# A two-layer graph transformer on one core: the first stage's typed projections by exact sort instead of by mask

## The chip, the cores and the metric

The kernel runs on one core of one Trainium2 chip. The core has a matrix engine (TensorE, PE in the profile), VectorE (DVE), ScalarE (ACT), GpSimd (POOL) and SyncE (SP), each with its own stream of instructions, and 16 DMA engines that move data between on-chip memory and DRAM. PEld is the matrix engine's loading of weights. The metric is the device time of one execution in microseconds (us); smaller is better. The kernel before takes 3468.3 us, the median of 9 runs between 3451.37 and 3474.05.

## The reference

A graph of 6250 nodes (128 features each, one of 16 node types) and 100000 edges (one of 32 edge types, sorted by destination) goes through two layers. What matters here is the start of a layer:

```python
def typed_linear(x, t, W):                      # W: 16 x 128 x 128, t: type of each node
    y_all = jnp.einsum('nd,tdo->nto', x, W)
    return jnp.take_along_axis(y_all, t[:, None, None], axis=1)[:, 0]

k = typed_linear(x, ntype, Wk).reshape(n, H, HS)   # H = 8 heads of HS = 16
q = typed_linear(x, ntype, Wq).reshape(n, H, HS)
v = typed_linear(x, ntype, Wv).reshape(n, H, HS)
kT = jnp.einsum('nhd,htdo->nhto', k, Watt)         # for each of 32 edge types
vT = jnp.einsum('nhd,htdo->nhto', v, Wmsg)
kw = kT[src, :, etype]
m  = vT[src, :, etype]
a  = jnp.einsum('ehd,ehd->eh', kw, q[dst]) * pri[:, etype].T / SQRT_D
att = edge_softmax(a, dst, n)
hag = segment_sum(m * att, dst)                    # then a typed linear, SiLU, skip, layer norm
```

After the two layers come a linear map and a last layer norm with a residual.

## The kernel before, in words

Nodes are padded to 49 blocks of 128 (6272 nodes). The program has a prologue, a first stage, and then the edges of layer 0 and of layer 1.

**First stage.** It writes the table `tabs[0]`: for every node and every one of the 32 edge types a row of 256 numbers (the node's k and v, already multiplied by the edge type's matrices). Per block of 128 nodes that is 4 MiB, in two pieces of 2 MiB ("table pieces", tile `st`, one for edge types 0 to 15 and one for 16 to 31, called `tg` 0 and 1), 98 pieces in all. `table_block` (L256) makes them: for each piece two halves (k, then v), for each half four products `tb` of 32 x 512 on TensorE (L268), each of which ScalarE (L275) or VectorE (L273, one in four) copies from PSUM into the piece. There are three `st` buffers. SyncE stores each piece to consecutive rows (L759).

The k and v of a block come from `linears0` (L721), which works on superblocks of 3 or 4 blocks: GpSimd loads the rows `hr` and a broadcast of the types `ntb` (L725, L727), TensorE transposes the rows, and then for each of the 16 types VectorE makes a copy of the superblock with all nodes of other types set to zero (`masked`, L238) and TensorE adds its products with that type's Wk and Wv (L739). So every node is multiplied 16 times for k and 16 times for v, and 15 of those products add zero. `linears0` of the next superblock is a generator: the loop at L755 to L773 takes one or two steps of it after each half of a table block.

**Ranking, beside the first stage.** `rank_order` (L452) is a second generator that the same loop advances. It first counts how many edges each node receives (`degrees`, L333: 46 chunks, each with a large comparison `ol` and a smaller one `oh` on VectorE, L348 and L351, and 17 small bf16 products on TensorE, L355). Then it ranks the nodes by type class and degree (VectorE with TensorE in turn, L457 to L656). Then come the "gathers" (L662 to L677): for each of 13 superblocks of the ranked order GpSimd gathers the edges' table indices `ell` (3 or 4 instructions, L664) and the nodes' rows `xr` (3 or 4, L673), and writes the rows out as `xrd` (L676), for which it first waits until the `xr` rows have landed. In the loop, `degrees` gets one step per half, the ranking two, the gathers one per two halves.

**Edges.** `edges` gathers table rows for the ranked nodes on GpSimd (L987, 1734 gathers over both layers), multiplies and reduces on VectorE, and writes layer 1's table `tabs[1]` with a GpSimd scatter per table piece (L1198, 100 of them) in between. The first gather of layer 0 waits until every piece of `tabs[0]` has landed.

**Order.** TensorE, VectorE, ScalarE and SyncE run their instructions in an order that the framework's scheduler makes from the program. GpSimd's order in the first stage and in the edges is the program's own (`manual_schedule`).

Of the kernel before, what the change touches and what calls it, by code (L numbers as in the profile page):

```python
# [9 lines left out]
F32 = mybir.dt.float32  # L10
# [8 lines left out]
P = 128  # L19
# [75 lines left out]

@with_exitstack
def kernel(
# [43 lines left out]
    PAD = P * EC + P  # L141
    assert D == P and H * HS == D and H == 8 and HS == 16 and EC % J == 0 and NP > N and L == 2
    assert max(KB) * H + P <= 512 and max(KB) <= P and min(KB) >= CH and NR >= NP and NB <= P and TY == NC * TC

# [145 lines left out]
    nti = pp.tile([P, NT], I32, name="nti")  # L290
    nc.sync.dma_start(dsti, dst[0:P])
# [3 lines left out]
    nc.sync.dma_start(nti, ntype.rearrange("(i p) -> p i", p=P))  # L295
# [23 lines left out]

    nc.vector.scalar_tensor_tensor(kvi, srci, float(RT), eti, op0=ALU.mult, op1=ALU.add)  # L320
# [12 lines left out]
    def degrees(got):  # L333

        loi = pp.tile([P, EC], I32, name="loi", tag="lo")
        hii = pp.tile([P, EC], I32, name="hii")
# [110 lines left out]
    with tc.tile_pool(name="tp", bufs=2) as tp, \  # L447
            tc.tile_pool(name="tlin", bufs=1, space=PSUM) as tlin, \
            tc.tile_pool(name="tnb", bufs=5, space=PSUM) as tnb, \
            tc.manual_schedule(engines={mybir.EngineType.Pool}):  # L450

        def rank_order():  # L452
# [231 lines left out]
            for l in range(L):  # L684
                sk = pp2.tile([P, TY], F32, name="sk")
                nc.scalar.dma_start(sk, skip[l:l + 1, :].to_broadcast([P, TY]))
                nc.scalar.activation(sk, sk, AF.Sigmoid)
                oa = pp.tile([P, NB, TY], F32, name="oa", tag="hii")
                nc.vector.tensor_tensor(oa, onehot, sk.unsqueeze(1).to_broadcast([P, NB, TY]),
                                        op=ALU.mult)  # L690
                nc.vector.tensor_reduce(alpha[:, l], oa, axis=AX.X, op=ALU.add)
                nc.vector.tensor_scalar(beta[:, l], alpha[:, l], -1.0, 1.0,
                                        op0=ALU.mult, op1=ALU.add)
                nc.vector.tensor_scalar(alpha[:, l], alpha[:, l], 0.5, None, op0=ALU.mult)
                yield
# [19 lines left out]
            nc.vector.tensor_copy(over, mt_ps[:, 0:1])  # L715
# [5 lines left out]
        def linears0(got, i0, k):  # L721

            n = k * P
            hr = tp.tile([P, SB, D], F32, name="hr")
            nc.gpsimd.dma_start(hr[:, :k], rows(x, i0, k))  # L725
            ntb = tp.tile([P, SB * P], I32, name="ntb")
            nc.gpsimd.dma_start(  # L727
                ntb[:, :n], ntype[i0 * P:i0 * P + n].unsqueeze(0).to_broadcast([P, n]))
            yield
            tr = tlin.tile([P, SB * P], F32, name="l0")  # L730
            for i in range(k):
                nc.tensor.transpose(tr[:, i * P:(i + 1) * P], hr[:, i, :], ident)
            hT = tp.tile([P, SB * P], F32, name="hT")
            nc.scalar.copy(hT[:, :n], tr[:, :n])
            ps = [tlin.tile([P, SB * P], F32, name=f"l{i}") for i in range(2)]
            yield
            for t, xm in masked(tp, range(TY), ntb, hT, n):
                for i in range(2):
                    nc.tensor.matmul(ps[i][:, :n], wkqv[:, i, t, :], xm[:, :n],  # L739
                                     start=(t == 0), stop=(t == TY - 1))  # L740
                yield
            kT, vT = (tp.tile([P, SB * P], F32, name=f"yT{i}") for i in range(2))
            nc.scalar.copy(kT[:, :n], ps[0][:, :n])
            nc.scalar.copy(vT[:, :n], ps[1][:, :n])
            got.append((kT, vT))
            yield

        load_later()


        got, stage = [], ""
        sbs = list(superblocks(NT))
        for _ in linears0(got, *sbs[0]):
            pass
        for s, (i0, k) in enumerate(sbs):  # L755
            beside = linears0(got, *sbs[s + 1]) if s + 1 < len(sbs) else iter(())
            for i in range(k):
                def store(tg, st, b=i0 + i):
                    nc.sync.dma_start(  # L759
                        tabs[0].rearrange("(n g t) c -> g n (t c)", g=TG, t=16)[  # L760
                            tg, b * P:(b + 1) * P, :],
                        st.rearrange("p t c -> p (t c)"))
                for half, _ in enumerate(table_block(tp, tnb, *got[s], i, (1,), 3, store)):
                    next(beside, None)
                    if half % 4 == 3:
                        next(beside, None)

                    if stage != "gathers" or half % 2:
                        stage = next(ranking, None)
                    if stage not in ("degrees", "gathers"):  # L770
                        stage = next(ranking, None)
            for _ in beside:
                pass  # L773
        for _ in ranking:
            pass
# [3 lines left out]
    def arm(fast):  # L779
# [527 lines left out]

        for l in range(L):
# [67 lines left out]
```

## Time and profile before

| | |
|---|---|
| median of 9 runs | 3468.3 us |
| the profiled execution | 3451.46 us, of which 3449.7 us are the profile's span |
| first product of a table piece | 52.86 us |
| first store of a piece issued / last issued | 57.1 / 798.1 us |
| `degrees` and ranking end, first `ell` gather | 558.4 us |
| last `xrd` written | 758 us |
| first gather of layer 0's edges | 810.24 us |
| TensorE busy, whole span | 1938.5 us (56%) |
| VectorE / ScalarE / GpSimd busy | 2164.7 (63%) / 978.6 (28%) / 2006.6 us (58%) |

An engine's busy time is the time in which one of its instructions runs; it says little on its own, because the stages have different limits. A table of windows gives, for each stretch of time, the busy time of each engine with its number of instructions, the clock that the matrix engine was granted (1 is full speed), the share of time in which the DMA engines were busy, and the rate that they moved. A row of the groups of instructions gives the line, engine, operation, output and input, the count, the busy time and the mean length of one in ns, and then the engine's idle time before them with what ended it. A row of the waits says which instruction waited for which, for how long in total, how often, and the longest.

### The profile page before, as it was taken

What the parts mean: (1) busy time and instruction counts of PE and PEld (TensorE: products, weight loads), DVE (VectorE), ACT (ScalarE), POOL (GpSimd) and SP (SyncE); (2) the same over time, 40 slices, a digit from 0 to 9 for tenths busy, and PEclk for the clock granted to TensorE, in tenths of its full rate; (3) what the DMA queues carried; (4) which work ended last, traced back from release to release, by engine and by line L of the source; (5) the groups of instructions that cost most, each with busy time, mean ns of one, the idle gap of its engine ahead of it and who ended that gap; (6) DMA issues with size and microseconds to landing.
All of it is one profiled execution on the core that took longest, in us unless ns stands there. A gap on an engine that the chain in (4) does not pass through costs nothing. (4 is left out here: it accounts for less than half of the span.)

```text
span 3449.7 us, 25373 instructions
## 1 busy us (share of the span) xinstructions
PE 1938.5 (56%) x7142; PEld 874.5 (25%) x7142; DVE 2164.7 (63%) x4496; ACT 978.6 (28%) x1594; POOL 2006.6 (58%) x2032
## 2 busy tenths in 40 slices
PE   6999999893066676786778777602112222131223
PEld 3444454332022232332233223201001111011111
DVE  5787786333665677666666765346656666566765
ACT  2444433452024313442344246301111111011111
POOL 0000003644767777777777676177767777777773
PEclk9999999995577677877678877755555555555555
DMA  7677655898347656875788488734433333343331
GB/s 198 275 299 288 275 238 213 321 374 272 98 132 274 221 191 224 302 275 190 241 289 306 158 294 333 303 107 113 109 99 109 111 111 107 110 117 110 111 106 48
DMA packets 201146, 694.53 MB, mean 201 GB/s; under 512 B 61382, under 2 KB 111896, under 8 KB 175946
## 3 DMA queue, kind: packets, MB, share of 16 engines
q0 software_dynamic: 105424, 448.83, 39.5%
q1 hardware_dynamic: 79182, 236.82, 17.8%
q10 hardware_dynamic: 16384, 7.11, 0.9%
q8 instruction: 60, 0.98, 0.1%
q14 instruction: 96, 0.79, 0.1%
HBM read 268.12 MB, written 429.48 MB: 202 GB/s over the span
## 5 line engine op out<-in xcount | busy, mean ns | idle before, releaser
L987 POOL DMA_INDIRECT kv<-tab,ell x1734 | 1709.4, 986 | 612.3 <-issue 473.1
L275 ACT COPY st<-tb 128x512 f32<-128x512 f32 (+1 forms) x976 | 680.7, 763 | 612.1 <-PE tb L268 520.4
L253 PE MATMUL nb<-ident,hag 128*128 128x128 f32 x100 | 25.7, 394 | 770.4 <-DVE hag L1037 753.0
L739 PE MATMUL l<-xm,wkqv 128*128 128x512 f32 (+1 forms) x832 | 385.6, 598 | 32.1 <-DVE xm L238 32.1
L999 DVE TENSOR_TENSOR kv<-kv,tb 128x512 f32<-128x512 f32 (+3 forms) x234 | 150.5, 645 | 379.9 <-DMA kv<-tab,ell 369.5
L999 DVE TENSOR_TENSOR kv<-kv,q 128x512 f32<-128x512 f32 (+3 forms) x234 | 151.5, 650 | 358.4 <-DMA kv<-tab,ell 350.6
L268 PE MATMUL tb<-bdv,kvT 32*128 32x512 f32 x800 | 266.1, 790 | 70.8 <-ACT st L275 70.3
L1003 DVE TENSOR_REDUCE a<-kv 128x32 f32<-128x512 f32 (+3 forms) x468 | 297.5, 638 | 2.2
L247 PE MATMUL nb<-xm,wa 128*128 128x384 f32 (+1 forms) x384 | 216.2, 727 | 84.6 <-DVE xm L238 84.4
L268 PE MATMUL tb<-bdk,kvT 32*128 32x512 f32 x800 | 242.5, 788 | 24.3 <-ACT st L275 23.9
L273 DVE COPY st<-tb 128x512 f32<-128x512 f32 (+1 forms) x208 | 149.1, 718 | 119.7 <-PE tb L268 96.5
L739 PEld LDWEIGHTS l<-xm,wkqv 128*128 128x128 f32 x832 | 148.7, 193 | 263.4 <-issue 197.8
L253 PEld LDWEIGHTS nb<-ident,hag 128*128 128x128 f32 x100 | 15.4, 195 | 787.8 <-issue 578.5
L238 DVE SCALAR_TENSOR_TENSOR xm<-ntb,nb 128x384 f32<-128x384 bf16 (+1 forms) x336 | 185.3, 591 | 43.9 <-PE nb L253 28.6
L238 DVE SCALAR_TENSOR_TENSOR xm<-ntb,hT 128x512 f32<-128x512 int32 (+1 forms) x208 | 133.5, 657 | 124.0 <-PE l L739 104.6
L1198 POOL DMA_INDIRECT tab<-st,row x100 | 113.3, 1133 | 145.6 <-ACT st L275 96.8
L727 POOL DMA_DIRECT2D ntb<-in_node_type_dram x13 | 7.3, 559 | 317.2 <-DVE xm L238 317.2
L247 PE MATMUL nb<-xm,wq 128*128 128x384 f32 (+1 forms) x192 | 100.5, 686 | 133.2 <-DVE xm L238 133.2
L268 PE MATMUL tb<-bdv,yT 32*128 32x512 f32 x784 | 169.3, 662 | 4.3 <-DVE st L273 2.2
L247 PEld LDWEIGHTS nb<-xm,wa 128*128 128x128 f32 x384 | 97.1, 265 | 201.4 <-DVE xm L238 115.2
L1132 PE MATMUL nb<-xm,wkqv 128*128 128x384 f32 (+1 forms) x288 | 127.0, 595 | 35.6 <-DVE xm L238 25.1
L889 ACT COPY tb<-q 128x128 f32<-128x128 f32 x50 | 13.4, 269 | 469.0 <-DVE sums L932 346.1
(243 smaller groups left out, 3002.6 us busy)
## 6 DMA issues: line engine op xcount, KB each, us to landing
tab<-st SPq DMA_DIRECT2D x98, 2048.0 KB, 6.8
kv<-tab,ell POOLq DMA_INDIRECT x1734, 2.8
hr<-xrd SPq DMA_DIRECT2D x30, 192.0 KB, 4.2
hr<-xrd SPq DMA_DIRECT2D x15, 256.0 KB, 4.5
xrd<-xr POOLq DMA_DIRECT2D x11, 256.0 KB, 4.8
hr<-in_x_dram POOLq DMA_DIRECT2D x10, 256.0 KB, 9.0
ntb<-in_node_type_dram POOLq DMA_DIRECT2D x10, 256.0 KB, 7.1
ntb<-typed SPq DMA_DIRECT2D x20, 96.0 KB, 3.2
```

The lines of the kernel that those rows point to most:

```text
L238: nc.vector.scalar_tensor_tensor(xm[:, :n], ntb[:, :n], float(t), hT[:, :n], op0=ALU.is_equal, op1=ALU.mult)
L247: nc.tensor.matmul(ps[:, :n], w[:, t, :], xm[:, :n], start=(t == types[0]), stop=(t == types[-1]))
L253: nc.tensor.transpose(tr[:, i * P:(i + 1) * P], src_of(i), ident)
L268: nc.tensor.matmul(pt[:, b], yT[s, i * P:(i + 1) * P], bd[s, tt, :], start=True, stop=True)
L273: nc.vector.tensor_copy(to, pt)
L275: nc.scalar.copy(to, pt)
L739: nc.tensor.matmul(ps[i][:, :n], wkqv[:, i, t, :], xm[:, :n], start=(t == 0), stop=(t == TY - 1))
L987: get = nc.gpsimd.indirect_dma_start(out=kv[:, j - j0, :], out_offset=None, in_=tabs[l][:], in_offset=bass.IndirectOffsetOnAxis(ap=ell[:, ...
L999: nc.vector.tensor_tensor(kk, kk, q.unsqueeze(1).to_broadcast([P, c, D]), op=ALU.mult)
L1003: nc.vector.tensor_reduce(a[:, j0:j1, :], kk.rearrange("p k (h d) -> p k h d", h=H), axis=AX.X, op=ALU.add)
L1132: nc.tensor.matmul(outs[j][:, :n], wkqv[:, j, t, :], xm[:, :n], start=(t == types[0]), stop=(t == types[-1]))
L1198: put = nc.gpsimd.indirect_dma_start(out=tabs[1].rearrange("(n t) c -> n (t c)", t=16), out_offset=bass.IndirectOffsetOnAxis(ap=row2[:, tg ...
```

## The change

The nodes are sorted by type before the first stage.

1. **Sort (new, in the prologue).** The types are loaded as rows (`ntr`) and transposed. A comparison `ty1` gives a 0/1 matrix node x type; two pairs of bf16 products give the number of nodes of each type per block and each node's place among its own type; a scan and sums give `place`, the node's place in the order by type. Comparisons `row1` and `col1` and 49 bf16 products turn that around into `inv`, the node that stands at each place. `rows1` holds the table's row numbers for the scatters. `first_t` is where each type begins. For each type a fixed range LO..HI of places is laid down beforehand in which it may begin (`windows_of_types`); `shift_t` is the beginning's distance from LO, and `odd` tells that a type begins outside its range or has over 512 nodes (then the kernel takes its general branch, which now makes the table anew).
2. **`linears0` works on a type.** GpSimd gathers the rows `xg` of the type's blocks that are new (1 to 4 indirect gathers). VectorE copies what overlaps with the last type's `hT`, `kT`, `vT` (three copies), GpSimd sets the rest of `kT` and `vT` to zero. TensorE transposes the new rows and makes one product for k and one for v on 512 columns that begin at an offset held in a register (`values_load` on TensorE, ScalarE and VectorE). ScalarE copies k, VectorE copies v to the same offset. The 16 masks and 30 of every 32 products are gone.
3. **Table pieces are scattered.** A block now holds nodes of the sorted order, so its rows lie apart in the table, and the piece is written by a GpSimd scatter (`put0`) instead of SyncE's store. A piece is put into GpSimd's order one piece late (`late`), so the order has one to a half of a block.
4. **Pace.** During `degrees` VectorE takes no copies of pieces (ScalarE takes all), and `degrees` gets two steps per half instead of one.
5. Small moves: `nti` comes from the transpose instead of a strided load; pools are opened earlier; two tiles share memory.

```diff
+def windows_of_types(n, pad, types, width):
+    low, high = [0], [0]
+    for t in range(1, types):
+        share = t / types
+        mean, dev = pad + n * share, math.sqrt(n * share * (1 - share))
+        low.append(max(0, int((mean - 5.0 * dev) // P) * P))
+        high.append(int(mean + 5.0 * dev) + 1)
+    ...
+    return low, high
...
-    nc.sync.dma_start(nti, ntype.rearrange("(i p) -> p i", p=P))
+    nc.sync.dma_start(ntr, ntype.rearrange("(i p) -> i p", p=P))
...
+    ty1 = tp.tile([P, TY, NT], BF16, name="ty1", tag="st", bufs=STB0)
+    nc.vector.tensor_tensor(ty1, ntf.unsqueeze(1).to_broadcast([P, TY, NT]), ..., op=ALU.is_equal)
...
+    nc.vector.tensor_tensor_scan(run_t, ones[:, 0:1].to_broadcast([P, wide]), cnt_t, 0.0, ...)
...
+    for i0 in range(0, NT, 17):
+        nc.vector.tensor_tensor(col1[:, sl, 1], ..., op=ALU.is_equal)
+        nc.vector.tensor_tensor(col1[:, sl, 0], col1[:, sl, 1], ..., op=ALU.mult)
+        nc.vector.tensor_scalar(col1[:, sl, 1], col1[:, sl, 1], rowf, None, op0=ALU.mult)
+        nc.vector.tensor_tensor(row1[:, sl], ..., op=ALU.is_equal)
+        for i in range(sl.start, sl.stop):
+            nc.tensor.matmul(inv_ps, row1[:, i], col1[:, i], start=(i == 0), stop=(i == NT - 1))
...
-        def linears0(got, i0, k):
-            nc.gpsimd.dma_start(hr[:, :k], rows(x, i0, k))
-            nc.gpsimd.dma_start(ntb[:, :n], ntype[...].unsqueeze(0).to_broadcast([P, n]))
-            ...
-            for t, xm in masked(tp, range(TY), ntb, hT, n):
-                for i in range(2):
-                    nc.tensor.matmul(ps[i][:, :n], wkqv[:, i, t, :], xm[:, :n], ...)
-                yield
+        def linears0(got, t):
+            b0, b1, _ = spans(t)
+            old = spans(t - 1)[1] if t else b0
+            n = b1 - old
+            if n:
+                xg = tp.tile([P, WB, D], F32, name="xg", bufs=1)
+                for i in range(n):
+                    nc.gpsimd.indirect_dma_start(out=xg[:, i, :], ..., in_=x, in_offset=...(inv...))
+            at = nc.values_load(shift_t[0:1, t:t + 1], engines=engines, ...)
+            yield
+            ...
+                for yT in (kT, vT):
+                    nc.gpsimd.memset(yT[:, WIN:HI[t + 1] - LO[t]], 0.0)
+            if t:
+                for to, of, end in ((hT, held[0], ...), (kT, held[1], ...), (vT, held[2], ...)):
+                    nc.vector.tensor_copy(to[:, :end - LO[t]], of[:, LO[t] - was:end - was])
+            yield
+            ...                                      # transposes, hT
+            for i, yT in enumerate((kT, vT)):
+                ps = tlin.tile([P, SB * P], F32, name=f"l{i}")
+                nc.tensor.matmul(ps, wkqv[:, i, t, :], hT[:, ds(at, WIN)], start=True, stop=True)
+                yield
+                if i:
+                    nc.vector.tensor_copy(yT[:, ds(at, WIN)], ps)
+                else:
+                    nc.scalar.copy(yT[:, ds(at, WIN)], ps)
+                yield
...
+        def put0(st, tg, b):
+            put = nc.gpsimd.indirect_dma_start(
+                out=tabs[0].rearrange("(n t) c -> n (t c)", t=16),
+                out_offset=bass.IndirectOffsetOnAxis(ap=rows1[:, tg, b:b + 1], axis=0),
+                in_=st.rearrange("p t c -> p (t c)"), in_offset=None, ...)
...
-                    nc.sync.dma_start(tabs[0].rearrange(...)[tg, b * P:(b + 1) * P, :], st...)
-                for half, _ in enumerate(table_block(tp, tnb, *got[s], i, (1,), 3, store)):
+                    late.append((st, tg, b))
+                share = () if stage in ("", "degrees") else (1,)
+                for half, _ in enumerate(table_block(tp, tnb, *got[t], b - b0, share, STB0, store)):
                     next(beside, None)
-                    if half % 4 == 3:
-                        next(beside, None)
+                    if half % 2 and len(late) > 1:
+                        put0(*late.pop(0))
                     if stage != "gathers" or half % 2:
                         stage = next(ranking, None)
-                    if stage not in ("degrees", "gathers"):
+                    if stage != "gathers":
                         stage = next(ranking, None)
```

The rest of the diff is the general branch's own making of the table, which does not run when `odd` is zero.

## The prediction

> **What bounds the kernel now.** I read the windows of the profile first, cut where the program's stages change. The columns are: stretch, its length, busy time (instructions) of TensorE, its weight loads, VectorE, ScalarE, GpSimd, then granted clock, DMA share, GB/s.
>
> ```profile
> 0.00:57.00 57.00, 28.16 (x101) 15.98 (x102) 28.11 (x111) 7.83 (x16) 5.20 (x15) 1.00 0.77 157
> 57.00:400.00 343.00, 332.02 (x1924) 144.71 (x1920) 265.26 (x282) 150.76 (x290) 8.52 (x13) 0.98 0.70 288
> 400.00:558.00 158.00, 150.54 (x803) 89.42 (x795) 118.29 (x228) 53.66 (x102) 0.54 (x1) 1.00 0.52 218
> 558.00:759.00 201.00, 187.08 (x697) 66.91 (x689) 89.08 (x185) 90.87 (x175) 118.83 (x119) 0.95 0.82 321
> 759.00:798.00 39.00, 36.40 (x139) 20.67 (x138) 12.15 (x20) 27.49 (x53) 0.00 (x0) 0.74 1.00 424
> ```
>
> The rows are prologue, `degrees`, ranking, gathers, and a tail without `linears0`. In the middle three TensorE is busy 93 to 97% of the time: it is the bound. Only in the tail do the DMA engines bound (share 1.00), with a store every 4.9 us. Then the groups of instructions for 57 to 810 us, and for 558 to 760 us on GpSimd:
>
> ```profile
> L739 PE MATMUL l<-xm,wkqv 128*128 128x512 f32 (+1 forms) x768 | 362.6, 604 | 12.7 <-DVE xm L238 12.7
> L275 ACT COPY st<-tb 128x512 f32<-128x512 f32 x583 | 305.2, 594 | 386.9 <-PE tb L268 378.3 <-DMA tab<-st 8.0
> L273 DVE COPY st<-tb 128x512 f32<-128x512 f32 x194 | 133.2, 687 | 89.8 <-PE tb L268 71.4 <-DMA tab<-st 11.4 <-ACT yT L744 6.0
> L348 DVE TENSOR_TENSOR ol<-lob,colb 128x2176 bf16<-128x2176 bf16 x44 | 106.6, 2422 | 21.1 <-PE ps L355 21.0
> ```
>
> ```profile
> L664 POOL DMA_INDIRECT ell<-kvs,start x50 | 52.5, 1050 | 138.5 <-DVE gap L643 123.5 <-issue 14.9
> L673 POOL DMA_INDIRECT xr<-in_x_dram,some x50 | 51.9, 1038 | 15.2 <-issue 15.2
> L676 POOL DMA_DIRECT2D xrd<-xr x13 | 10.4, 802 | 51.4 <-DMA xr<-in_x_dram,some 34.2 <-issue 17.2
> ```
>
> L739, half of TensorE's time, is what the change takes away; it will not all become time, because the next limits stand close. L348 shows VectorE's price of `degrees`. The last three are a chain on GpSimd: a gather costs its mean plus 0.3 us of "issue", and each `xrd` waits for its rows (51.4 us in 13). Last, a window of layer 0's edges with six scatters of table pieces and no gather, and the DMA issues with size and time to landing:
>
> ```profile
> 2200.00:2230.00 30.00, 18.29 (x72) 6.12 (x72) 12.07 (x11) 9.83 (x13) 5.85 (x6) 0.69 0.94 393
> ```
>
> ```profile
> tab<-st SPq DMA_DIRECT2D x98, 2048.0 KB, 6.8
> ...
> tab<-st,row POOLq DMA_INDIRECT x100, 8.3
> ```
>
> A scattered piece thus drains in 2.097 MB / (393/0.94 GB/s) = 5.0 us and lands 1.5 us later than a stored one.
>
> **The change part by part.** The first gather of the edges started at 810.2 us; I work out when it starts now, as a chain of stages.
>
> *Sort, before `degrees`.* VectorE waits for the edge types until 12.5 us as before. Then about 32 short operations at 0.14 us (the spacing of L306 to L516), seven on 781 to 784 columns at 0.97 (L324; the scan up to 1.7), four copies or sums of 392 columns at 0.55: 14.5 us. Then `col1`, nine at up to 1.02 (L351), `row1` at 2.42, 2.42 and 2.1, and the weight scaling 1.4: 17.5 us. The reply of TensorE, `inv`, and the branch (2.1 us idle at L339) take 4. With 1.5 us of hand-overs `degrees` begins at about 50 us instead of 27. Bounds: 44 (the short ones overlap, the 8-us wait for `nti` goes) and 62 (the weights come late).
>
> *`degrees`.* The built order puts 92 comparisons, 15 hand-over copies, 5 `vT` copies and 5 register loads on VectorE here. A pair `ol`, `oh` takes 2.33 + 0.94 = 3.27 us by the starts in the timeline at 162.60 to 166.48, so 46 pairs 150; conversions 2.2; copies of 5734 columns 7; `vT` 5 x 0.69; loads 5 x 1.0 (L1322); a first wait for gathered rows 5. Together 173 us, end at 223. Bounds 160 (no waits) and 195 (1 us more per pair after the first 20). Beside it a half needs on ScalarE 4 x 0.594 = 2.4 us, on TensorE 2.1, and on the DMA 2.5, all under 3.27, so VectorE is the limit. Doubling the steps is why this part halves. That VectorE gives its copies away saves 46 x 0.69 us there and costs nothing on ScalarE while 2.4 < 3.27; without the cover 0.
>
> *Ranking.* The groups L457 to L656 and L681 sum to 87.7 us on VectorE. With 31 copies of pieces (21.2), 7 hand-over copies (3), 3 `vT` and loads (5): 117. Of VectorE's 40 idle us in this window before, 17 waited for L739 and go; 23 waited for ranking products and stay. 140 us, end at 363 (before: 558). Bounds 117 and 160, the old stage.
>
> *Gathers.* Here GpSimd becomes the limit: the built order has in its list 100 gathers, 13 `xrd`, 25 scatters, 15 `xg` and 10 memsets, one after another. 100 x 1.345 = 134.5; 13 x 1.1 = 14; scatters 25 x (1.133 + 0.3) = 36; `xg` 15 x 1.34 = 20; memsets 3.5 (0.21 for 128 columns). The wait before `xrd` is the unknown. Its rows now queue behind a scatter of 5.0 us in the same software queue; the scatter lands 8.3 us after its issue, and four gathers take 5.4 us to issue, so 2.8 us remain: 36. Bounds: 2.0, the least of the 13 waits of before, and 7.7, the longest. I take 2.8, near the low end, because the stores of the other queue are gone; what queues behind the waiting `xrd` is the next scatter, and behind that a piece buffer. 244 us, end at 607 (before 759). Bounds 225 and 308.
>
> *Rest.* 35 scatters remain, and nothing but the DMA limits: 35 x 5.0 = 175, three type changes at 2 us (`xg` behind a scatter), landing 3. End 791. Bounds 174 (at the store's 4.87) and 205.
>
> *Costed at nothing.* TensorE keeps 64 product records x 0.6 = 39 us, the transposes, and 49 sort products; cover is VectorE, then GpSimd, then DMA. SyncE's 98 stores go; nothing waited for SyncE. The 38 scatters issued before the gathers (54 us of GpSimd) lie in its idle time (it was busy 9 of 501 us). The edges have the same order on GpSimd, so I take them as unchanged, within 5 us either way.
>
> Sum: 791 against 810.2, 19 us less. The profiled execution took 3451.5 us and would take 3432; it was near the fastest of the runs, 17 under the median, so on the median 3468.3 - 19 = **3449**.
>
> Two rules of the Trainium skill speak against this. First the rows: scatters took 0.974 us at least, 1.017 in the median and 1.133 in the mean, with VectorE busy beside them about half the time. "SBUF — State Buffer", section "SBUF: two separate sides", says that GpSimd cannot write descriptors while VectorE copies fp32 within on-chip memory, and the hand-over copies are such copies. If all 30 of them after `degrees` hit a descriptor at 0.5 us each, 15 of the 19 us would go; no run here shows that. The second row is the 424 GB/s of the tail. "DMA: Bandwidth & Descriptors", section "Specifications", gives a limit of about 358 GB/s of DRAM per core. By it a piece takes 5.9 us, the rest 205 and the change loses 11 us; the trace's 4.9 and 5.0 decide.
>
> **The rivals.**
>
> *The gather chain grows (slower).* If a row waits for two pieces ahead of it, not one, the wait is 2.8 + 5 = 7.8 us, 13 x 5 = 65 us more: 46 slower than before, 3514. It decides from 4.3 us per wait (19/13 more than 2.8), and the mean before was 3.95, so this is near. Against it: two scatters are 5 us of gathers apart.
>
> *VectorE waits for TensorE in `degrees` (slower).* Each pair needs products that stand behind four `tb` in TensorE's order, and those behind a piece buffer. At 1 us a pair this costs 46 us, 3495; for it speak the 21.1 us that L348 waited before, against it that TensorE then had L739 between.
>
> *Both chains run bare (faster).* Ranking without its 23 us, waits of 2.0 (10), gathers at 0.95 + 0.3 (10): 43 more, 3406.
>
> *The general branch runs.* The change's ranges are five deviations wide and types hold 356 to 444 nodes of 512 allowed; excluded. That all of L739's 363 us become time is excluded too: 98 pieces x 5.0 = 490 us of DMA would then be the whole stage.
>
> **How the numbers follow.** About 0.3%, 10 us, is what a measurement of this kernel tells from no change. Forecast 0.45, its own range 3425 to 3475 (the sort, ranking and rest bounds): 0.29 faster, 0.11 same, 0.05 slower. Gather chain 0.21 and VectorE's waits 0.14: slower, but 0.03 of it the same, where they come in part. Bare chains 0.20: faster. Together faster 0.49, same 0.14, slower 0.37. The range 3400 to 3515 reaches to both sides' rivals.
>
> **What would show it.** Right: no L739 masks; `degrees` at 3.3 us a pair with VectorE over 90% busy; the first `ell` at 363; GpSimd without a gap but the `xrd` waits until 607; then DMA share near 1.0 with a scatter every 5 us; first edge gather at 791. Wrong: `xrd` waits above 4.3 us; VectorE waiting for `ps` at each `ol`; scatters above 1.4 us; TensorE waiting for `xg` at each type; or a DMA share under 0.9 after 607.

## The result, and the profile after

The changed kernel took 3447.2 us in the median of 20 runs (3436.9 to 3465.0), against 3468.1 us in 62 runs of the kernel before. The ratio is 0.994, 95% interval 0.993 to 0.995: faster by 0.6%, about 21 us. The forecast was 3449 us, 19 us less. One execution of a run below, 3669.3 us with `xrd` written by SyncE, is 8% above its five neighbours and is left out of the numbers.

The profiles look different at first sight. The profiled execution of the changed kernel took 3457.3 us (span 3455.4), that of the kernel before 3451.5: about 6 us *more*. The first gather of the edges starts at 808.0 us instead of 810.2. So the forecast was met on the medians, while the chain of stages that it was worked out from ended 17 us later than the 791 us predicted. Both have to be explained.

The windows of the changed kernel, cut at its own stages. The columns are the same as before the change: stretch, its length, busy time (instructions) of TensorE, its weight loads, VectorE, ScalarE and GpSimd, then granted clock, DMA share, GB/s. The rows are the sort, `degrees`, ranking, gathers, and the rest.

```profile
0.00:42.68 42.68, 6.45 (x56) 4.90 (x56) 33.83 (x97) 2.13 (x5) 3.31 (x42) 1.00 0.90 165
42.68:227.60 184.92, 136.69 (x1192) 69.18 (x1192) 161.81 (x148) 98.22 (x194) 120.31 (x52) 0.76 0.61 248
227.60:385.05 157.45, 144.03 (x690) 88.42 (x690) 104.53 (x208) 55.21 (x105) 24.94 (x27) 0.78 0.56 232
385.05:623.50 238.45, 171.03 (x467) 84.39 (x464) 57.68 (x146) 88.37 (x171) 150.10 (x163) 0.55 0.68 253
623.50:808.00 184.50, 153.44 (x532) 82.08 (x528) 51.34 (x81) 104.71 (x202) 41.61 (x47) 0.69 0.99 409
```

`degrees` and ranking shrank from 343 and 158 us to 185 and 157, the gathers are longer (238 instead of 201) with TensorE busy only 72% of the time, and a rest of 184 us has appeared in which the DMA is full (0.99). GpSimd, busy 8.5 us in the 343 us of `degrees` before, is now busy 120 us in it. That is far more than its 52 gathers, scatters and memsets should need. The groups of the first stage show why:

```profile
L898 POOL DMA_INDIRECT tab<-st,rows x98 | 155.2, 1583 | 278.3 <-ACT st L298 224.2 <-issue 17.3 <-DVE rl L702 15.5
L852 POOL DMA_INDIRECT xg<-in_x_dram,inv x49 | 66.9, 1365 | 56.0 <-DVE few L633 38.7 <-issue 11.6 <-PE l L874 2.3
L790 POOL DMA_DIRECT2D xrd<-xr x13 | 10.5, 804 | 46.7 <-DMA xr<-in_x_dram,some 41.2 <-issue 5.4
```

The first number behind the bar is busy time, the second the mean duration in ns. A scatter should take about 1.0 us (the median of layer 1's scatters before is 1.017); the mean is 1.583. The timeline of GpSimd, and that of VectorE for the same stretch (start, duration, then engine, line, operation, and in brackets the idle time before and what ended it), show one of those that lift the mean:

```profile
148.45 1.15 POOL L898 DMA_INDIRECT tab<-st,rows  x1 [6.27 <-ACT st L298]
153.77 23.09 POOL L898 DMA_INDIRECT tab<-st,rows  x1 [4.17 <-ACT st L298]
177.17 1.00 POOL L852 DMA_INDIRECT xg<-in_x_dram,inv  x1 [0.30 <-issue]
```

```profile
171.73 1.02 DVE L468 TENSOR_TENSOR oh<-hib,colb 128x833 bf16<-128x833 bf16 x1
172.67 2.42 DVE L465 TENSOR_TENSOR ol<-lob,colb 128x2176 bf16<-128x2176 bf16 x1
175.00 1.02 DVE L468 TENSOR_TENSOR oh<-hib,colb 128x833 bf16<-128x833 bf16 x1
187.98 2.50 DVE L465 TENSOR_TENSOR ol<-lob,colb 128x2176 bf16<-128x2176 bf16 x1 [11.96 <-PE ps L472]
```

One scatter lasts 23.1 us, from 153.77 to 176.86, through seven pairs of `ol` and `oh` and two short hand-over copies on VectorE without a break. It ends 0.84 us after VectorE stops at 176.02. VectorE stops because it waits for TensorE, whose products stand behind table pieces (TensorE waits 11.93 us for ScalarE), whose buffers stand behind this scatter (ScalarE waits 15.99 us for one); the wait costs VectorE 11.96 us. Two more follow each other, 15.75 us at 87.71 and 6.83 us at 103.76, with a VectorE wait of 4.32 us behind them. The first of these ends at 103.46 without a stop of VectorE, 0.93 us after VectorE began to copy `vT` out of PSUM (L885). That VectorE's own comparisons hold up the scatter is so far only a reading of two timelines.

### The profile page after: what moved, and what is told of

The parts are those of the page before. It is cut to its first block, busy times and chain, and to the rows that moved or that the text cites. A ratio compares the mean times of both kernels' runs of the same rounds, so it can differ in the third digit from the quotient of the medians.

```text
span 3455.4 us, 24065 instructions
## 1 busy us (share of the span) xinstructions
PE 1817.3 (53%) x6428; PEld 864.8 (25%) x6428; DVE 2060.5 (60%) x4345; ACT 996.8 (29%) x1634; POOL 2219.7 (64%) x2213
## 5 line engine op out<-in xcount | busy, mean ns | idle before, releaser
L298 ACT COPY st<-tb 128x512 f32<-128x512 f32 (+1 forms) x1024 | 704.7, 759 | 591.2 <-PE tb L291 335.0
L1155 DVE TENSOR_TENSOR kv<-kv,q 128x512 f32<-128x512 f32 (+3 forms) x234 | 151.7, 650 | 374.6 <-DMA kv<-tab,ell 364.1
L291 PE MATMUL tb<-bdv,vT 32*128 32x512 f32 x784 | 312.6, 917 | 97.3 <-ACT st L298 95.4
L898 POOL DMA_INDIRECT tab<-st,rows x98 | 155.2, 1583 | 278.3 <-ACT st L298 224.2
L296 DVE COPY st<-tb 128x512 f32<-128x512 f32 (+1 forms) x160 | 116.4, 729 | 292.4 <-DMA tab<-st,rows 145.8
L291 PE MATMUL tb<-bdk,kT 32*128 32x512 f32 x784 | 261.7, 935 | 3.3 <-DVE st L296 3.3
L270 PE MATMUL nb<-xm,wa 128*128 128x384 f32 (+1 forms) x384 | 207.6, 702 | 91.2 <-DVE xm L261 91.0
L261 DVE SCALAR_TENSOR_TENSOR xm<-ntb,nb 128x384 f32<-128x384 bf16 (+1 forms) x336 | 185.2, 591 | 36.2 <-PE nb L276 22.9
L291 PEld LDWEIGHTS tb<-bdv,vT 32*128 32x128 f32 x784 | 109.1, 253 | 188.4 <-ACT st L298 166.9
L1045 ACT COPY tb<-q 128x128 f32<-128x128 f32 x50 | 13.4, 269 | 470.3 <-DVE sums L1088 347.2
L1288 PE MATMUL nb<-xm,wkqv 128*128 128x384 f32 (+1 forms) x288 | 126.8, 592 | 39.1 <-DVE xm L261 28.6
L1307 PE MATMUL nb<-xm,wkqv 128*128 128x384 f32 (+1 forms) x288 | 131.0, 615 | 13.5 <-DVE xm L261 13.5
```

The source lines that it names most:

```text
L261: nc.vector.scalar_tensor_tensor(xm[:, :n], ntb[:, :n], float(t), hT[:, :n], op0=ALU.is_equal, op1=ALU.mult)
L270: nc.tensor.matmul(ps[:, :n], w[:, t, :], xm[:, :n], start=(t == types[0]), stop=(t == types[-1]))
L291: nc.tensor.matmul(pt[:, b], yT[s, i * P:(i + 1) * P], bd[s, tt, :], start=True, stop=True)
L296: nc.vector.tensor_copy(to, pt)
L298: nc.scalar.copy(to, pt)
L898: put = nc.gpsimd.indirect_dma_start(out=tabs[0].rearrange("(n t) c -> n (t c)", t=16), out_offset=bass.IndirectOffsetOnAxis(ap=rows1[:, t ...
```

## Experiments on the long scatters

**The column numbers in PSUM.** If a comparison with two operands in SBUF keeps GpSimd out, one operand in PSUM should let it in. The edit, which takes the bank from the `tb` tiles:

```diff
-    tnb = prep.enter_context(tc.tile_pool(name="tnb", bufs=5, space=PSUM))
+    tnb = prep.enter_context(tc.tile_pool(name="tnb", bufs=4, space=PSUM))
+    cps = prep.enter_context(tc.tile_pool(name="cps", bufs=1, space=PSUM))
+    colp = cps.tile([P, P], F32, name="colp")
+    nc.vector.tensor_copy(colp, colf)
...
-                                    colb.unsqueeze(1).to_broadcast([P, J, P]), op=ALU.is_equal)
+                                    colp.unsqueeze(1).to_broadcast([P, J, P]), op=ALU.is_equal)
...
-                                    colb[:, :NT].unsqueeze(1).to_broadcast([P, J, NT]),
+                                    colp[:, :NT].unsqueeze(1).to_broadcast([P, J, NT]),
```

> In the changed kernel, the column numbers that `ol` and `oh` of `degrees` are compared with lie in PSUM as fp32 instead of in SBUF as bf16, so that a comparison has one operand from SBUF and not two; for the bank, the product tiles `tb` have four buffers instead of five. Theory (VectorE's instructions with two operands in SBUF keep GpSimd from writing the descriptors of a scatter until VectorE stops or does something else): no scatter or gather on GpSimd before 240 us longer than 3 us (now 15.8, 23.1 and 6.8), VectorE's waits of 4.3 and 12.0 us for `ps` at L472 gone, `degrees` 16 us shorter if a comparison keeps its 2.33 us, first gather of the edges near 792 instead of 808 us, ratio to before 0.990. Rival (the long scatters wait for room in a queue full of rows): scatters above 10 us stay, ratio 0.994. Rival (four `tb` are too few): VectorE or ScalarE wait more for `tb`, ratio above 0.995.

**The control.** The same fp32 numbers and the same four buffers, with the numbers in SBUF. The two kernels differ only in where `colp` lies:

```diff
-    cps = prep.enter_context(tc.tile_pool(name="cps", bufs=1, space=PSUM))
-    colp = cps.tile([P, P], F32, name="colp")
+    colp = pp.tile([P, P], F32, name="colp")
```

> The control of the columns in PSUM: the same fp32 column numbers, the same four buffers of `tb`, but the numbers lie in SBUF, so that each comparison has two operands from SBUF again. Theory (the second operand from SBUF is what keeps GpSimd out): scatters above 10 us are back, the mean of the 98 scatters is near 1.5 us (1.583 with bf16 in SBUF, 0.998 with fp32 in PSUM), `degrees` ends 15 to 20 us later than 207.4 us, ratio to before 0.993 to 0.997. Rival (fp32 against bf16, or four `tb` buffers, shortened the scatters): mean near 1.0 us, end near 207 us, ratio 0.991.

Measured: with the numbers in PSUM 3438.0 us, ratio to before 0.992 (0.990 to 0.994); with the same numbers in SBUF 3466.5 us, 1.000 (0.998 to 1.001). The groups, in PSUM and then in SBUF:

```profile
L901 POOL DMA_INDIRECT tab<-st,rows x98 | 97.8, 998 | 313.5 <-ACT st L298 260.4 <-issue 16.2 <-DVE rl L705 15.5
L468 DVE TENSOR_TENSOR ol<-lob,colp 128x2176 bf16<-128x2176 bf16 x46 | 110.8, 2408 | 1.1 <-PEq L500 1.1
```

```profile
L900 POOL DMA_INDIRECT tab<-st,rows x98 | 162.6, 1659 | 293.0 <-ACT st L298 240.1 <-issue 16.0 <-DVE rl L704 15.5
L467 DVE TENSOR_TENSOR ol<-lob,colp 128x2176 bf16<-128x2176 bf16 x46 | 111.1, 2415 | 14.4 <-PE ps L474 13.3 <-PEq L499 1.0
```

The comparison itself costs the same (2.41 and 2.42 us). The scatters fall from a mean of 1.659 us to 0.998, none in all of the 98 is longer than 1.3 us, and VectorE's wait for `ps` of 13.3 us is gone. `degrees` ends at 207.4 us instead of 237.5. In the control, scatters of 23.0, 20.3 and 8.0 us are back. Only the place of one operand differs, so it is the second operand in SBUF that keeps GpSimd from finishing its scatter; the rivals of a full queue and of fp32 against bf16 fall.

The traces fit this one by one. In the five profiles that have them (both of the changed kernel, the control, and the runs with `xrd` on SyncE and with plain stores below), 15 scatters and gathers of GpSimd last over 6 us. Ten end 0.8 to 0.9 us after VectorE stopped, and five end 0.9 us after it began a copy of `vT` out of PSUM. The hand-over copies from SBUF to SBUF that ran inside them, up to two in each, ended none.

The rival of the four `tb` buffers came in part. The control, which has them too, is 19 us slower than the changed kernel, outside the range expected of it, and its rest takes 195 us. Of the 20 us that `degrees` gained over the changed kernel, 14 reached the first gather of the edges (794.1 us); six went in the rest, 190.5 us instead of 184.5. VectorE's copies of pieces over the first stage, in the changed kernel and with the numbers in PSUM:

```profile
L296 DVE COPY st<-tb 128x512 f32<-128x512 f32 x148 | 101.9, 689 | 267.5 <-DMA tab<-st,rows 145.8 <-PE tb L291 118.9 <-PE l L874 2.7
L296 DVE COPY st<-tb 128x512 f32<-128x512 f32 x148 | 102.1, 690 | 275.1 <-PE tb L291 156.9 <-DMA tab<-st,rows 118.0
```

They wait more for `tb` products and less for piece buffers. In the rest alone, VectorE and ScalarE waited 105.0 and 54.6 us for `tb` instead of 65.1 and 21.5, and 11.8 and 11.2 us for buffers instead of 43.9 and 36.7; the DMA share was 0.95 instead of 0.99. So the rest is no longer the DMA's. In that part the two kernels differ in nothing but the number of `tb` buffers, but no run changes that number alone.

The Trainium skill, "SBUF — State Buffer", section "SBUF: two separate sides", says that a pair of ports is shared by VectorE and GpSimd as an exclusive lock, taken also by a VectorE operation with two inputs from SBUF against a GpSimd operation that reads SBUF. The runs agree: a scatter takes its row numbers `rows1` from SBUF. They add how long it can last: 23.1 us, while VectorE ran sixteen instructions back to back.

**The same kernel again.** The changed kernel without any edit, profiled a second time.

> The changed kernel, unchanged, profiled a second time. Theory (which scatters lose against VectorE is a matter of a few hundred nanoseconds, so it differs between executions): long scatters again, but in other places or of other lengths than 15.8 us at 87.7 and 23.1 us at 153.8; the first `ell` moves by 5 to 20 us against 385.1 and the first gather of the edges by the same against 808.0. Rival (the schedule fixes them): the same scatters of the same length within 1 us, first `ell` within 3 us of 385.1.

Measured: 3451.7 us. There are long scatters again, of 24.0 us at 106.6 and 20.9 us at 200.6, and none near 87.7 or 153.8. So which scatter is caught can differ between executions, and both pay for it. The ends moved less than expected: first `ell` at 382.0 instead of 385.1, first gather of the edges at 806.0 instead of 808.0.

## Experiments on the gather chain

**`xrd` written by SyncE**, whose queue the change has emptied:

```diff
-                nc.gpsimd.dma_start(rows(xrd, i0, k), xr[:, :k])
+                nc.sync.dma_start(rows(xrd, i0, k), xr[:, :k])
```

> In the changed kernel, the 13 writes of `xrd` are issued by SyncE instead of GpSimd. Theory (the gathers are a chain on GpSimd, and its waits for `xr` stand in it): the 46.7 us of waits and 13 x 1.1 us of issue leave the chain, so the stretch from first `ell` to last gather falls from 238 to about 180 us, and with 35 pieces left at 5.0 us the first gather of the edges comes near 750 us, ratio 0.977. Rival (the stretch is set by the pieces that are interleaved in it: TensorE was busy 158 of its 220 us): scatters wait for ScalarE's pieces instead, the stretch falls to 205 or not at all, ratio 0.985 to 0.994. Rival (the DMA is the limit of the whole stage): the stretch is shorter but the rest longer by as much, ratio 0.994.

Measured: 3388.2 us, ratio 0.976 (0.975 to 0.978). First gather of the edges at 749.9 us. Its windows of the gathers and of most of the rest:

```profile
378.00:550.00 172.00, 143.51 (x440) 69.62 (x433) 55.71 (x144) 81.99 (x158) 132.00 (x141) 0.64 0.88 335
550.00:740.00 190.00, 174.70 (x564) 91.56 (x559) 53.73 (x82) 111.51 (x214) 48.93 (x55) 0.63 0.95 393
```

The stretch from the first `ell` (378.3 us) to the end of the last gather (559.3) is 181 us instead of 234 (238 with the last `xrd`, which GpSimd then issued), and the DMA share in it rises from 0.68 to 0.87. The waits stood in the chain, at their full price.

**The same edit in the kernel before.**

> The kernel before, with nothing changed but that SyncE writes `xrd` instead of GpSimd. In the changed kernel the same edit was worth 58 us. Theory (before the change TensorE and its products were the limit while the gathers ran, busy 187 of 201 us, and only the change turned the gather chain into the limit): the 50 to 60 us of waits go from GpSimd, but what TensorE has to do remains, so the gain is no more than TensorE's idle time, 14 us in the first profile of before and 29 in the second, ratio 0.990 to 0.997. Rival (the gather chain was the limit before, too): first gather of the edges near 765 us, ratio 0.983 or less.

Measured: 3501.0 us, ratio 1.010 (1.008 to 1.012), slower. Both theories fall. First gather of the edges at 863.3 us instead of 810. The waits of this kernel in 558 to 860 us:

```profile
ACT st L275 <- DMA tab<-st: 83.5, 12, 25.1
DVE st L273 <- DMA tab<-st: 78.8, 12, 23.3
```

The columns are total, number and longest wait. In the kernel before, ScalarE and VectorE waited 8.0 and 11.4 us for a piece buffer; now it is 84 and 79, up to 25 us at a time. SyncE's queue stores the pieces in this kernel. A write of `xrd` that waits in that queue for its gathered rows (123.7 us in all) holds up the stores behind it, and so the buffers. The rows of the queue give start, duration and how many in a row were merged:

```profile
633.82 20.12 SPq L676 DMA_DIRECT2D xrd<-xr  x3
654.05 0.44 SPq L759 DMA_DIRECT2D tab<-st  x1
663.53 0.36 SPq L676 DMA_DIRECT2D xrd<-xr  x1
664.00 18.34 SPq L759 DMA_DIRECT2D tab<-st  x5
```

GpSimd's gathers end at 714.5 us here, earlier than before, and the table is still finished later. So the edit is worth 58 us in the one kernel and costs 1% in the other. It pays where the change has moved the stores to GpSimd.

**Plain stores.** The changed kernel with the scatter taken out:

```diff
-            put = nc.gpsimd.indirect_dma_start(
-                out=tabs[0].rearrange("(n t) c -> n (t c)", t=16),
-                out_offset=bass.IndirectOffsetOnAxis(ap=rows1[:, tg, b:b + 1], axis=0),
-                in_=st.rearrange("p t c -> p (t c)"), in_offset=None,
-                bounds_check=NP * TG - 1, oob_is_err=False)
+            put = nc.sync.dma_start(
+                tabs[0].rearrange("(n g t) c -> g n (t c)", g=TG, t=16)[
+                    tg, b * P:(b + 1) * P, :],
+                st.rearrange("p t c -> p (t c)"))
```

> In the changed kernel, each table piece is stored by SyncE in one contiguous transfer, as in the kernel before, instead of scattered by GpSimd; the rows are then left in the order of types and are not put back at their nodes. Theory (the scatter costs VectorE 16 us of waits in `degrees` by being locked out, and 25 places of 1.3 us in the gather chain): `degrees` without VectorE waits above 3 us, GpSimd's gathers before 240 us still 1 to 3 us, first `ell` near 369 instead of 385, last gather near 575 instead of 623, first gather of the edges near 757, ratio 0.985. The `xrd` waits tell a second thing: if the rows of a gather queue behind scattered pieces, they fall from 3.6 to about 2.0 us; if not, they stay between 3 and 4. Rival (scattering is as good as storing, since TensorE and ScalarE set `degrees` and the DMA the rest): ratio 0.992 to 0.996.

Measured: 3417.9 us, ratio 0.985 (0.983 to 0.987), as expected in the total, while the stages came out otherwise. `degrees` ends at 214.6 us, 13 earlier, the longest VectorE wait for `ps` in it being 4.9 us. The first `ell` comes at 374.6 us instead of 369, the last gather ends at 601.6 us instead of 575, and the first gather of the edges starts at 772.3 instead of 757. The `xrd` waits did not fall to 2.0 us: they rose to 70.4 us in 13, 5.4 each. The prediction had it that rows queue behind a scatter; with no scatters at all they wait longer, beside stores from SyncE. So a scatter ahead of them is not needed for that wait. What pieces in flight add is seen in the next run, one step per half: its last three waits, with no piece left to store, are 2.2, 2.2 and 2.9 us. The gathers of `x` by type still ran against VectorE's comparisons, and they were caught as the scatters had been: expected at 1 to 3 us, four of them took 13.0, 30.2, 13.4 and 23.8 us. A caught gather holds no piece buffer.

## Experiments on the steps per half

**One step per half**, the last part of the change undone:

```diff
-                share = () if stage in ("", "degrees") else (1,)
+                share = (1,)
...
-                    if stage != "gathers":
-                        stage = next(ranking, None)
```

> In the changed kernel, the last part of the change is undone: one step of `degrees` and ranking per half of a piece instead of two, and VectorE takes its quarter of the copies in all stages. Theory (two steps per half shorten `degrees`, but the pieces that they leave over cost 5.0 us each at the end): `degrees` holds 46 pieces instead of 23; a half costs VectorE 3.27/2 + 0.69 = 2.3 us, the DMA 2.5 and TensorE's four `tb` up to 3.6, so it takes 240 to 330 us instead of 182; 23 fewer pieces at the end give back 115 us. First gather of the edges between 750 and 840 us, middle 795, ratio 0.990. With VectorE less dense in two-operand instructions, scatters above 10 us should be gone by the lock theory. Rival (the stage is as long as the chain of steps): the order of the steps costs its full price, 60 to 150 us more in `degrees` and nothing given back, ratio above 1.01.

Measured: 3419.3 us, ratio 0.985 (0.984 to 0.987). First gather of the edges at 768.8 us. `degrees` ends at 345.0 us, 117 us later; in exchange, the last piece is issued at 707 us, and none is left when the gathers end at 765. The windows of `degrees`, cut at 300 us, of its end with the first of the ranking, of the rest of the ranking, and of the gathers:

```profile
46.00:300.00 254.00, 232.06 (x1330) 101.44 (x1329) 195.10 (x219) 130.58 (x248) 119.27 (x79) 0.78 0.76 313
300.00:440.00 140.00, 138.21 (x707) 68.50 (x703) 87.72 (x150) 76.33 (x147) 44.05 (x43) 0.77 0.87 358
440.00:546.00 106.00, 98.48 (x521) 54.66 (x521) 80.36 (x159) 55.49 (x107) 28.09 (x32) 0.95 0.80 332
546.00:690.00 144.00, 101.56 (x297) 52.02 (x295) 36.53 (x93) 56.04 (x108) 86.04 (x90) 0.56 0.73 279
690.00:769.00 79.00, 7.99 (x22) 4.07 (x22) 3.74 (x6) 6.55 (x14) 41.72 (x46) 0.50 0.50 168
```

The DMA works at 0.73 to 0.87 from the first piece on. In the changed kernel it works at 0.56 to 0.68 for 580 us, and the pieces left over are then stored at 0.99 with nothing beside them. Two steps per half made `degrees` short by putting off the pieces, and the pieces cost more at the end. The edit also gives VectorE its quarter of the copies back, and no run tells the two apart. The longest scatter is now 3.3 us, as expected: VectorE's copies of pieces out of PSUM stand between the comparisons.

**Combinations.** Columns in PSUM with `xrd` on SyncE:

> The changed kernel with both changes that helped it: column numbers in PSUM, `xrd` written by SyncE. Theory (they act in different stages, so the gains add: 14 us of the profiles and 58): first gather of the edges at 808 - 14 - 58 = 736 us, ratio 0.972. Rival (the DMA, at a share of 0.88 to 0.95 from 378 us on with `xrd` on SyncE, takes back what a shorter `degrees` gives): no better than `xrd` on SyncE alone, 750 us, ratio 0.976.

Measured: 3380.3 us, ratio 0.975 (0.973 to 0.978); first gather of the edges at 744.7 us, so 5 of the 14 us came through. The interval overlaps that of `xrd` alone: the rival's number is nearer, but not its cause. The gathers begin and end 12.7 us earlier than with `xrd` alone (365.7 and 546.6 us), and the rest takes 198 us instead of 191, at a DMA share of 0.93 instead of 0.97. Again the copies wait for `tb` (VectorE 110.8 us instead of 73.9) and not for the DMA.

One step per half with `xrd` on SyncE:

> The changed kernel with one step of `degrees` and ranking per half, VectorE's quarter of the copies in all stages, and `xrd` written by SyncE. With one step, the gathers alone ran from 546 to 765 us with a DMA share of 0.73 and then 0.50, and no pieces were left. Theory (GpSimd is then the limit, and its waits of 52.2 us and 13 issues of 1.1 us leave the chain; the DMA's work up to the edges is 584 us by its shares and doesn't bind): first gather of the edges at 700 to 715 us, ratio 0.967. Rival (the last pieces and the DMA set the end): 740 us or more, no better than 0.976.

Measured: 3361.4 us, ratio 0.968 (0.966 to 0.971), first gather at 715.9 us, just past the upper end of the theory. This is faster than both kernels of this case, by 107 us against before and by 86 against the changed one.

All three:

> The changed kernel with one step per half, `xrd` written by SyncE and the column numbers in PSUM. Theory (with one step per half, scatters were still 1.44 us in the mean, but VectorE waited for products only 16 us in 17 pieces, of which a part is locked-out scatters): 5 to 12 us less than without the columns in PSUM, first gather of the edges near 700 us, ratio 0.965. Rival (four `tb` buffers cost as much, or GpSimd's delays are hidden where VectorE is not the limit): no difference of over 0.2% between the two.

Measured: 3359.8 us, ratio 0.969 (0.966 to 0.971), first gather at 716.8 us: no difference, the rival. The scatters fell from 1.430 to 1.010 us in the mean and `degrees` ended 10 us sooner (335.1 instead of 345.0 us), but the gathers began no sooner (548.9 instead of 546.1). Up to there ScalarE waited 216 us for `tb` instead of 183, and VectorE 50 instead of 33: the four buffers again.

**What the products alone were worth.** The kernel before with one type instead of sixteen:

```diff
-            for t, xm in masked(tp, range(TY), ntb, hT, n):
+            for t, xm in masked(tp, range(1), ntb, hT, n):
...
-                                     start=(t == 0), stop=(t == TY - 1))
+                                     start=True, stop=True)
```

> The kernel before, with L739's loop over the sixteen types cut to type 0 alone: one mask and two products per group of four blocks, so nodes of other types get k and v of zero (that part of the computation is left out). It prices what the change could have had without a sort, with plain stores, and with one step per half. Theory (with the products gone, VectorE, the DMA and then GpSimd bound, and sort, scatter and the doubled step cost the change most of its gain): the kernel with one step and the sort reached the edges at 769 us, of which about 20 us are the sort and 38 us are GpSimd's scatters and type gathers between the ranking and the edges, so the first gather of the edges comes at about 690 to 715 us against 810, ratio 0.966 to 0.971. Rival (the stage is bound otherwise, by copies, DMA and GpSimd, and L739 alone was worth little): 780 us or later, ratio 0.99 or more.

Measured: 3355.4 us, ratio 0.968 (0.966 to 0.970), in the middle of the theory's range, and first gather at 715.8 us, at its upper end. Taking fifteen of the sixteen masks and products away was worth 3.2%, 112 us, not all of L739's 363. The change kept 0.6%. With one step per half and `xrd` on SyncE it is as fast as this kernel, sort and scatter included. This kernel still has its own `xrd` waits on GpSimd, 81.9 us, so 3.2% is not the most that the products could give.

## Why the profiles and the medians disagree

The kernel before, profiled a second time:

> The kernel before, unchanged, profiled a second time, since its first profiled execution was the fastest of its runs (3451.5 against a median of 3468). Theory (the spread lies in the long part behind the first stage, whose order of work is the same in all kernels): the first gather of the edges is again within 3 us of 810.2 us, and the part behind it, 2639.5 us in the first profile, is longer, by about 15 us if the execution is an ordinary one. Rival (the spread lies in the first stage, in TensorE's clock): the part behind keeps within 5 us of 2639.5, and the first gather of the edges comes near 825 us.

Measured: 3466.5 us, an ordinary execution. The first gather of the edges starts at 827.6 us, and the part behind it takes 2637.1 us against 2639.5: the theory falls, and the rival is right on the place. The clock is not where it begins. Up to the gathers the two profiles agree within 2 us (first `ell` at 558.4 and 560.2), with the same granted clock (0.98, then 1.00), and in the first 40 us of the gathers, at 0.96 in both, the second `xrd` already waits 6.8 us instead of 2.4. One stretch of the gathers, 720 to 760 us, in the first and in the second profile:

```profile
720.00:760.00 40.00, 40.00 (x155) 13.85 (x154) 15.34 (x23) 19.05 (x37) 19.16 (x19) 1.00 0.92 376
```

```profile
720.00:760.00 40.00, 30.80 (x108) 10.87 (x108) 14.25 (x21) 13.09 (x25) 25.02 (x25) 0.81 0.70 266
```

In the second TensorE is idle for 9 of the 40 us. The `xrd` waits are 61.3 us instead of 51.4, and the next rows `hr` (L725) are issued by GpSimd right behind a waiting `xrd`, 6, 12 and 16 us later than in the first profile. TensorE's weight loads wait for them 29.2 us instead of 11.2; these 18 us are the 17.4 between the two first gathers. The first profile was an execution in which this went well. Against 827.6 us, the changed kernel's 806.0 and 808.0 are 20 to 22 us less. The medians say 20.8. The changed kernel's own profiles are not ordinary either: at 3457.3 and 3451.7 us they lie 10 and 4.5 above its median, and where those microseconds lie in them is open.

## Why the prediction was right, point by point

The predicted stages were 50, 173, 140, 244 and 184 us; measured were 42.7, 184.9, 157.5, 238.4 and 184.5. The differences, -7.3, +11.9, +17.5, -5.6 and +0.5, add up to the 17 us by which 791 was missed. The forecast on the median held because it took a difference of 19 us from a profile that itself was 17 us ahead of an ordinary execution. The order of the stages and their limits were right in the main: VectorE in `degrees`, GpSimd's chain in the gathers, the DMA in the rest. In absolute terms the new chain was 17 us too short, and the old one, taken as it stood in the profile, 17 us too short as well. That agreement of two errors was luck.

- *Sort, 50 us:* 42.7, just under the lower bound of 44; which of its terms was too large was not worked out.
- *`degrees`, 173 us:* 184.9 and, in the second profile, 190.1. The pair at 3.27 us is right. The step said that TensorE, DMA and ScalarE all lie under it; left out was that the comparisons keep GpSimd's scatters from ending. The rival in which VectorE waits for TensorE came in part: 17.1 us in three waits instead of 46, and by way of the scatters. The prediction did set the skill's rule beside the trace, but for the hand-over copies; those copies run in the PSUM version, too, and its scatters take 0.998 us. It is the comparisons.
- *Ranking, 140 us:* 157.5 and 149.5. This is the largest miss, and its step is "TensorE costed at nothing". VectorE was busy 104.5 us, less than the 117 worked out, but idle 52.9 instead of 23. Four of these 30 us are a reading: the 17 us of waits for L739 are of a longer window, and in 400 to 558 us they and the wait for `hT` are 12.8. The rest are waits for TensorE. The three longest, after and then before (total, number, longest):

```profile
DVE rl L735 <- PE ps L747: 15.0, 12, 3.0
DVE oc L591 <- PE ps L600: 10.2, 12, 1.1
DVE st L296 <- PE tb L291: 9.7, 8, 1.5
```

```profile
DVE rl L621 <- PE ps L633: 8.7, 10, 1.9
DVE st L273 <- PE tb L268: 3.4, 8, 0.7
DVE oc L477 <- PE ps L486: 3.0, 6, 1.8
```

  They are 34.9 us, against 15.1 for the same three operations before. In this stage the granted clock was 0.78, against 1.00 before, and the same 264 records of `tb` products kept TensorE busy for 62.5 us instead of 45.5. The products that were left became slower. In the second profile, with the clock at 0.83 and VectorE busy for 104.3 us, the stage is 8 us shorter. Why the clock fell was not tested.
- *Gathers, 244 us:* 238.4. The wait taken at 2.8 us was 3.6 (46.7 us in 13), under the point of 4.3 from which the rival decides. A gather was cheaper, 0.97 + 0.3 us instead of 1.345. The mechanism given for the wait, a row behind a scatter in the same queue, was not borne out by the run with plain stores, where it is 5.4 us without any scatter.
- *Rest, 184 us:* 184.5, and 185.2 in the second profile. Piece by piece at 5.0 us, with the DMA at 0.99. By the lower DRAM limit that the prediction weighed, an estimate, it would have been 205 us for the pieces alone, some 214 with type changes and landing; the measured 409 GB/s decide for the trace's own row.
- *Edges unchanged within 5 us:* 2647.4 and 2643.8 us behind the first gather, against 2639.5 and 2637.1; some 7 us longer, while the other kernels of the changed form gave 2630 to 2644. This is about the size of the spread and stays open.
- *Rivals:* the gather chain grew to below its deciding point; bare chains did not come; no general branch ran. One sign that the prediction had named for being wrong did come, scatters above 1.4 us in the mean (1.583), and VectorE was busy 87.5% of `degrees` and not over 90; the median held all the same.

## What to carry to other kernels

When a large part of the bound engine's work goes, look first at the order that was made for the old bound: here products of 363 us went, which was worth 112 us in the kernel before, and the change got 21. Another step schedule and another queue for one write brought it 86 more. A write that waits belongs on a queue with nothing urgent behind it, and which queue that is can change with the very edit at hand (58 us gained in one kernel, 1% lost in the other). Take a difference from a profile only after a second profile has said how far the same kernel's stages move by themselves.

## What was unexpected of the hardware

A scatter issued by GpSimd took 0.998 us in the mean while VectorE's comparisons had one operand in PSUM, and up to 23 us (mean 1.659) while both lay in SBUF, with VectorE's own instructions no slower (2.41 and 2.42 us). A single VectorE copy out of PSUM between the comparisons was enough to let it end, 0.9 us after that copy began; copies within SBUF were not. And the clock granted to TensorE was 0.76, 0.78 and 0.55 in `degrees`, ranking and gathers, where with the old products it had been 0.98, 1.00 and 0.95; a `tb` product that had taken 0.66 to 0.67 us in the mean up to 810 us took 0.92 to 0.94 up to 820.
